# Two graph layers on one core: sums by a stationary identity instead of accumulated transposes

## The chip, the core and the metric

The kernel runs on one core of a Trainium2 chip. The metric is the device time in microseconds (us) of one launch. Every line number below is a line of the kernel before, as its profile gives it. The engines are called PE (TensorE's matmuls), PEld (TensorE's weight loads), DVE (VectorE), ACT (ScalarE), POOL (GpSimd) and SP (SyncE).

## The reference

The input x has 8 batches of 2048 nodes with 256 features; adj is a symmetric 2048 x 2048 matrix, nearly all zero, with ones on the diagonal. Two layers follow each other, each with a residual and a layer norm around it. Cut to what matters:

```python
# layer 0, four heads of 64, keys in chunks of 256
q, k, v = x @ Wq.T + bq, x @ Wk.T + bk, x @ Wv.T + bv
scores = clip(einsum(q, k) / sqrt(64), -10, 10)
scores = where(mask == 0, -10, scores)
attn = softmax(scores)                 # within each chunk of 256 keys
ctx = sum over chunks of attn @ v
out = layernorm(ctx @ Wo.T + bo + x) * gamma + beta
x = layernorm(x + out)
# layer 1, four heads of 64
Wh = x @ W
e = leaky_relu(s_src[i] + s_dst[j]);  alpha = softmax(where(adj, e, -inf))
x = layernorm(x + elu(alpha @ Wh))
```

## The kernel before

The kernel makes use of the few ones in adj. A first part builds, for each node, the list of its neighbours, sorts the nodes by the number of neighbours and cuts them into NT = 16 tiles of 128 nodes. Tile t is processed with CAPS[t] neighbour slots: 24, 14, 13, 12, 11, 11, 10, 10, 9, 9, 8, 8, 7, 7, 6, 5, in all 164. A slot is one neighbour of each of the 128 nodes; its rows are fetched by one indirect DMA (`gather`, line 489, issued by POOL). Two slots lie together in a unit, a buffer of a ring of 14; a tile with an odd number of slots has a last unit with one slot. The 16 tiles have 86 units.

Layer 0 works on G = 2 batches at a time, so there are four groups g, and 64 pairs of group and tile. For each pair:

- `scores0` multiplies the gathered keys with the node's own query row. For about a third of the units VectorE both multiplies and reduces (`reduced`, lines 554 and 556). For the others (62 of a group's 86 units, 248 in all) VectorE multiplies (line 547), with the product laid out as NJ = 8 pieces of 2 slots x 64 columns, and TensorE adds the eight pieces by eight accumulating transposes into the bank `pr` (line 566). ScalarE copies that to `prT` (lines 572 and 574) and a matmul with the 0/1 matrix `sel` (line 576) adds the remaining 8 values of each slot and head, back in the layout of nodes by slots, into a bank `tf`.
- `softmax0` clamps the scores (line 590 from `tf`, line 593 for those that VectorE made) and turns them to weights `al`.
- `context0` multiplies the gathered values by the weights, on VectorE (line 501) or for the last quarter of the units on ScalarE (line 507), and `summed` (line 514) adds all slots by accumulating transposes, four of 128 x 128 a slot, into a bank `acc`, which ScalarE copies to `cT` (line 626).
- `finish0` multiplies by Wo (line 635) and does the norms; `rows1` transposes the rows (line 307, bank `tf`, copied to `x1T` by line 658) and makes layer 1's table (line 663). `tables` makes the next group's tables of queries, keys and values (lines 336 to 391, banks `tk`).

Layer 1 works on pairs of groups, four batches at once, so there are 32 pairs of p and tile, and each slot is summed in two halves k of 512 columns. `softmax1` makes the weights, `context1` multiplies and sums as in `context0`, into two banks `acc`, and copies both to `hT` (line 722). `finish1` transposes `hT` back (line 734, bank `mf`), takes the exponential (line 737) and the rest of elu (lines 738 and 741), and does the norm. The result is scattered by POOL (lines 748 and 753) in the step after.

The order is written out in a list `seq`: layer 0 of groups 0 and 1, then groups 2 and 3 with one tile of layer 1's first pair after every second tile, then the second pair alone. The first pair's tiles come with 7, 6, 9, 10, 11, 24, 10, 8, 7, 5, 8, 9, 11, 14, 13 and 12 slots, the second pair's with 5, 7, 8, 9, 10, 11, 12, 14, 24, 13, 11, 10, 9, 8, 7 and 6. A step's functions are called in the order scores0 of this tile, then (where one is due) finish1 of the last and context1 of the next tile of layer 1, then rows1, finish0, tables, softmax0 and context0. A planner places each engine's instructions from there, so those of neighbouring functions lie between each other; where they share a buffer, the order of the calls holds.

PSUM has eight banks of 128 x 512 f32. Before, they go to `acc` 2, `tf` 2, `tk` 2, `pr` 1 and `mf` 1.

Of the kernel before, what the change touches and what calls it, by code (L numbers as in the profile page):

```python
# [45 lines left out]
def edge_lists(tc: tile.TileContext, pool, bank, adj, const, ident, rec_d, B, between):  # L46
# [24 lines left out]
    for it in range(NT):  # L71
# [8 lines left out]
        if it % 4 == 0:  # L80
            kp = bank("acc")
# [92 lines left out]
def sparse_path(ctx: ExitStack, tc: tile.TileContext, keep, x, adj, Wq, bq, Wk, bk, Wv, bv, Wo, bo, gamma, beta, W, a,  # L174
# [38 lines left out]
    def by_part(v):  # L213
        return v.rearrange("p (j h d) -> p h j d", h=H, d=DP)


    sel = const.tile([P, P // DP], F32, name="sel")
    nc.gpsimd.memset(sel, 1.0)
    nc.gpsimd.affine_select(out=sel, in_=sel, compare_op=ALU.is_ge, fill=0.0, base=0, pattern=[[-DP, P // DP]],
                            channel_multiplier=1)  # L220
    nc.gpsimd.affine_select(out=sel, in_=sel, compare_op=ALU.is_ge, fill=0.0, base=DP - 1, pattern=[[DP, P // DP]],
                            channel_multiplier=-1)
# [9 lines left out]
    def bank(tag, bufs=2):  # L232

        return ps.tile([P, 512], F32, tag=tag, name=tag, bufs=bufs)
# [296 lines left out]
    def scores0(g, t):  # L531
# [6 lines left out]
        ps_sc = bank("tf")[:, 0:GH * S].rearrange("p (s e) -> p s e", e=GH)  # L538
# [21 lines left out]
        for i in range(1, npe, 4):  # L560
            some = units[i:min(i + 4, npe)]
            pr = bank("pr", 1).rearrange("p (k r) -> p k r", r=P)
            for k, (u, s0, n) in enumerate(some):
                prod = product(i + k)
                for j in range(NJ):
                    nc.tensor.matmul(pr[0:n * W8, k, :], prod[:, j // (NJ // UNIT), j % (NJ // UNIT), :], ident, is_transpose=True,  # L566
                                     start=(j == 0), stop=(j == NJ - 1), skip_group_check=True)
            m = len(some)
            prT = work.tile([P, 4, P], F32, tag="prT", name="prT", bufs=1)
            full = m - 1 if some[-1][2] < UNIT else m  # L570
            if full:
                nc.scalar.copy(prT[:, 0:full, :], pr[:, 0:full, :])
            if full < m:
                nc.scalar.copy(prT[0:W8, full, :], pr[0:W8, full, :])
            for k, (u, s0, n) in enumerate(some):
                nc.tensor.matmul(ps_sc[:, s0:s0 + n, :], prT[0:n * W8, k, :], sel[0:n * W8, 0:n * GH],  # L576
                                 start=(s0 == UNIT), stop=(k == m - 1 and i + m == npe), skip_group_check=True)
        for unit in units[npe:]:
            reduced(*unit)
        st0[g, t] = ps_sc, sc, min(S, UNIT * npe)  # L580
# [5 lines left out]
    def softmax0(g, t):  # L586
        S = CAPS[t]
        n = GH * S
        ps_sc, sc, sp = st0.pop((g, t))
        nc.vector.tensor_scalar(sc[:, :, UNIT:sp], ps_sc[:, UNIT:sp, :].rearrange("p s e -> p e s"), -10.0, 10.0, op0=ALU.max,  # L590
                                op1=ALU.min)
        for some in [sc[:, :, 0:UNIT]] + ([sc[:, :, sp:]] if sp < S else []):
            nc.vector.tensor_scalar(some, some, -10.0, 10.0, op0=ALU.max, op1=ALU.min)
# [16 lines left out]
    def context0(g, t):  # L610
# [3 lines left out]
        acc = bank("acc").rearrange("p (c r) -> p c r", r=P)  # L614
# [38 lines left out]
    def rows1(g, t):  # L653

        o = st0.pop((g, t))
        pt = transposed(o.rearrange("p b f -> p (b f)"), "tf", 2)
# [13 lines left out]
    got1, st1 = {}, {}  # L670

# [31 lines left out]
    def context1(p, t):  # L703
# [3 lines left out]
        accs = [bank("acc").rearrange("p (c r) -> p c r", r=P) for _ in range(2)]  # L707
# [5 lines left out]
        for i, (u, s0, n) in enumerate(units):  # L713
            for k in range(2):
# [3 lines left out]
                summed(accs[k], part, s0 == 0, s0 + n == S)  # L718
        hTs = []
        for k in range(2):  # L720
            hT = work.tile([P, G * KC, P], F32, tag="hT", name="hT")
            nc.scalar.copy(hT, accs[k])
            hTs.append(hT)
        xr = work.tile([P, 2, GF], F32, tag="xr", name="xr")
        nc.sync.dma_start(xr, x1_d[p][t * P:(t + 1) * P])
        st1[p, t] = hTs, xr

    def finish1(p, t):
        hTs, xr = st1.pop((p, t))
        sums = small.tile([P, 2 * G], F32, tag="sums1", name="sums1")  # L730
        for k, hT in enumerate(hTs):
# [79 lines left out]
    for k, (layer, i) in enumerate(seq):  # L811
# [6 lines left out]
        if layer == 0:  # L818
# [15 lines left out]
            if tables_first:  # L834
                fetch(k + 1)
# [451 lines left out]
```

## Time and profile before

| | |
|---|---|
| runs shown | 2379.63, 2385.73, 2388.16 us; median 2385.73 us |
| profiled execution | 2397.55 us, its span 2395.8 us |
| mean granted TensorE clock | 0.885 |
| busy: PE, DVE, ACT, POOL | 1900.4, 1833.5, 1409.0, 1505.0 us |
| DMA | 669.10 MB, mean 279 GB/s |

The busy time of an engine is the time in which at least one of its instructions runs. TensorE's matmuls overlap each other, so the mean duration of one (some 290 ns for a transpose) is longer than the distance from one to the next. The granted clock is the share of TensorE's full clock that its throttle let through. The span falls into stages: preparation and the neighbour lists to about 210 us, the first steps of layer 0 to about 440, layer 0 of groups 0 and 1 to about 1090, group 2 with layer 1 and the last projections to about 1448, group 3 with layer 1 to about 1952, and layer 1 alone to the end.

### The profile page before, as it was taken

The numbers are of one execution on the slowest core, as the hardware profiler recorded it, in microseconds if no ns is written. First come the engines' busy times: TensorE is split into PE (matmuls) and PEld (weight loads), VectorE is DVE, ScalarE is ACT, GpSimd is POOL, SyncE is SP. The second block draws the span as 40 slices with busy tenths as digits, with TensorE's granted clock in tenths as the row PEclk, the third lists the DMA queues.
The fourth block names the chain that finished last, engine by engine and source line by source line (L and its number), as shares of the span: only waits on it lengthen the run. The fifth ranks groups of instructions, "written<-read, shape, count | busy, mean of one in ns | idle before, by whom it ended". The sixth has DMA issues, their size and how long they took to land. (4 is left out here: it accounts for less than half of the span.)

```text
span 2395.8 us, 38844 instructions
## 1 busy us (share of the span) xinstructions
PE 1900.4 (79%) x11946; PEld 1622.0 (68%) x11946; DVE 1833.5 (77%) x4099; ACT 1409.0 (59%) x5036; POOL 1505.0 (63%) x1230
## 2 busy tenths in 40 slices
PE   7686889889899898999988885888678786664764
PEld 5565677778778787777876774776566675554653
DVE  6864587877588988588988886887788887775775
ACT  4573455546566555655565665664356677665766
POOL 3125455672666676376668856774677685787883
PEclk9897899899999999999998997987878987877887
DMA  7737877795889798598879977896679896786884
GB/s 259 242 137 272 265 270 281 260 346 209 316 287 320 260 334 319 212 388 298 302 258 353 360 281 238 285 321 221 230 274 326 306 319 248 278 310 231 302 296 154
DMA packets 239982, 669.10 MB, mean 279 GB/s; under 512 B 43688, under 2 KB 70059, under 8 KB 237719
## 3 DMA queue, kind: packets, MB, share of 16 engines
q0 software_dynamic: 156800, 505.01, 60.1%
q1 hardware_dynamic: 79248, 151.55, 17.2%
q10 hardware_dynamic: 3718, 9.97, 1.3%
q8 instruction: 98, 1.61, 0.3%
q14 instruction: 118, 0.96, 0.1%
HBM read 612.79 MB, written 126.36 MB: 309 GB/s over the span
## 5 line engine op out<-in xcount | busy, mean ns | idle before, releaser
L489 POOL DMA_INDIRECT u<-kv_d,idx x656 | 810.2, 1235 | 436.4 <-PE acc L514 185.7
L514 PE MATMUL acc<-ident,u 128*128 128x128 f32 x5248 | 713.4, 291 | 157.0 <-DVE u L501 89.0
L514 PEld LDWEIGHTS acc<-ident,u 128*128 128x128 f32 x5248 | 637.5, 151 | 220.7 <-DVE u L501 133.2
L489 POOL DMA_INDIRECT u<-wh_d,idx x328 | 416.5, 1270 | 148.2 <-issue 76.4
L566 PE MATMUL pr<-ident,u 128*128 128x128 f32 (+1 forms) x1984 | 287.0, 295 | 78.7 <-DVE u L547 77.2
L501 DVE TENSOR_TENSOR u<-u,al 128x1024 f32<-128x1024 f32 x280 | 334.5, 1234 | 1.5
L566 PEld LDWEIGHTS pr<-ident,u 128*128 128x128 f32 (+1 forms) x1984 | 245.4, 151 | 110.8 <-DVE u L547 104.6
L547 DVE TENSOR_TENSOR u<-u,qx 128x1024 f32<-128x1024 f32 (+1 forms) x248 | 302.0, 1218 | 18.3 <-DMA u<-kv_d,idx 15.1
L501 DVE TENSOR_TENSOR u<-u,z 128x1024 f32<-128x1024 f32 x266 | 314.4, 1212 | 0.6
L507 ACT ACTIVATE u<-u,z 128x64 f32<-128x64 f32 x1008 | 262.0, 337 | 25.0 <-DVE z L700 17.1
L507 ACT ACTIVATE u<-u,al 128x64 f32<-128x64 f32 x800 | 209.1, 342 | 23.2 <-DVE al L607 22.3
L663 PE MATMUL mf<-wa,x1T 128*128 128x264 f32 x512 | 167.6, 455 | 23.1 <-ACT x1T L658 14.8
L351 POOL TENSOR_TENSOR xt<-xt,beta_r 128x1024 f32<-128x1024 f32 x32 | 77.1, 2410 | 143.1 <-PE tk L336 126.3
L385 PE MATMUL tk<-wq,xT 128*128 128x256 f32 x512 | 145.2, 397 | 24.4 <-ACT kvs L379 24.4
L451 ACT ACTIVATE nm<-sums 128x2 f32<-128x2 f32 (+1 forms) x160 | 32.4, 202 | 221.3 <-DVE sums L641 122.6
L372 PE MATMUL tk<-wkv,xT 128*128 128x256 f32 x512 | 151.7, 410 | 12.9 <-ACT xC L341 12.6
L635 PE MATMUL mf<-wo,cT 128*128 128x256 f32 x512 | 148.4, 415 | 6.3 <-ACT whs L666 5.3
L376 PE MATMUL tk<-wkv,xC 128*128 128x256 f32 x512 | 144.5, 399 | 0.0
L663 PEld LDWEIGHTS mf<-wa,x1T 128*128 128x128 f32 x512 | 101.7, 218 | 59.7 <-ACT x1T L658 23.6
L455 ACT ACTIVATE sq<-o,nm 128x256 bf16<-128x256 f32 x256 | 129.7, 507 | 5.3
L554 DVE TENSOR_TENSOR u<-u,qx 128x1024 f32<-128x1024 f32 (+1 forms) x96 | 116.0, 1214 | 16.6 <-DMA qx<-qx_d,node 7.1
L590 DVE TENSOR_SCALAR sc<-tf 128x64 f32<-128x64 f32 (+5 forms) x64 | 14.0, 218 | 138.2 <-PE tf L576 138.2
(168 smaller groups left out, 3254.0 us busy)
## 6 DMA issues: line engine op xcount, KB each, us to landing
kv_d<-kvs SPq DMA_DIRECT2D x48, 512.0 KB, 6.0
wh_d<-whs SPq DMA_DIRECT2D x64, 260.0 KB, 5.8
xt<-in_x_dram SPq DMA_DIRECT2D x64, 256.0 KB, 4.8
qx_d<-xt SPq DMA_DIRECT2D x32, 512.0 KB, 4.4
qx_d<-qs SPq DMA_DIRECT2D x64, 256.0 KB, 5.8
x_d<-o SPq DMA_DIRECT2D x64, 256.0 KB, 5.2
xr<-x_d SPq DMA_DIRECT2D x32, 512.0 KB, 4.9
u<-kv_d,idx POOLq DMA_INDIRECT x656, 6.5
```

Source lines behind the costliest of these rows:

```text
L372: nc.tensor.matmul(pm[:, 0:F], xT[:, b * KC + kc, rows], wkv[:, kc, 0:F], start=(kc == 0), stop=False, skip_group_check=True)
L376: nc.tensor.matmul(pm[:, F:], xC[:, b * KC + kc, rows], wkv[:, kc, F:], start=False, stop=(kc == KC - 1), skip_group_check=True)
L385: nc.tensor.matmul(qb, xT[:, b * KC + kc, rows], wq[:, kc, :], start=(b == 0 and kc == 0), stop=False, skip_group_check=True)
L455: nc.scalar.activation(sq, src[:, k, :], AF.Square, bias=nm[:, k:k + 1], accum_out=m2[:, k:k + 1])
L489: nc.gpsimd.indirect_dma_start(out=u[:, k, 0:width], out_offset=None, in_=table, in_offset=bass.IndirectOffsetOnAxis(ap=idx[:, t, s0 + k:s ...
L501: nc.vector.tensor_tensor(pv, pv, av, op=ALU.mult)
L507: nc.scalar.activation(pe, pe, AF.Copy, scale=al[:, e, s0 + k:s0 + k + 1])
L514: nc.tensor.matmul(acc[:, c, :], part[:, k, c * P:(c + 1) * P], ident, is_transpose=True, start=first and k == 0 and c == 0, stop=last and ...
L547: nc.vector.tensor_tensor(prod.rearrange("p k j (s w) -> p k j s w", w=W8), u[:, :, 0:GF].rearrange("p s (k j w) -> p k j s w", k=UNIT, w=W8),
L566: nc.tensor.matmul(pr[0:n * W8, k, :], prod[:, j // (NJ // UNIT), j % (NJ // UNIT), :], ident, is_transpose=True, start=(j == 0), stop=(j ...
L635: nc.tensor.matmul(po[:, b, :], cT[:, b * KC + kc, :], wo[:, kc, :], start=(b == 0 and kc == 0), stop=False, skip_group_check=True)
L663: nc.tensor.matmul(pw[:, 0:F + 2 * H], xT[:, b * KC + kc, :], wa[:, kc, :], start=(kc == 0), stop=(kc == KC - 1))
```

## The change

Both kinds of sums change from accumulated transposes (the data stationary, the identity moving) to plain matmuls with the identity stationary and the data moving, which leave the sum untransposed.

- Scores: the eight pieces of a unit are added by eight matmuls of 128 columns (64 for a unit with one slot) into the unit's own columns of a bank `pr`, up to four units side by side. The copies `prT`, the matrix `sel` and its matmul are gone. In `softmax0` VectorE adds the remaining 8 values straight from PSUM, one `tensor_reduce` for each bank, into `sc`; one clamp for the whole tile takes the place of two or three.
- Layer 1: a slot's half of 512 columns is added by one matmul. The banks are left as they are until `finish1`, which reads them where it read `mf`; the copies `hT` and the transposes of line 734 are gone, and the exponential has a buffer of its own.
- Layer 0's context sums (`summed` from `context0`) stay as they were.
- PSUM: `acc` has one bank, which `rows1` uses too; `tf` is gone; `pr` has two; `a1` is new with two, for layer 1's sums. While group 3 runs and after it, when `tables` no longer needs `tk`, layer 1's tiles use `a1` and `tk` in turn.

The diff, without the lines that only move a bank of the preparation and remove `sel`:

```diff
@@ -535,7 +529,7 @@
         sc = small.tile([P, GH, S], F32, tag="sc", name="sc")
 
         npe = 1 + len(units) - len(units) // 3
-        ps_sc = bank("tf")[:, 0:GH * S].rearrange("p (s e) -> p s e", e=GH)
+        sums = []
         W8 = GH * DP
         qv = q.rearrange("p (k j w) -> p k j w", k=UNIT, w=W8).unsqueeze(3)
 
@@ -559,25 +553,18 @@
         reduced(*units[0])
         for i in range(1, npe, 4):
             some = units[i:min(i + 4, npe)]
-            pr = bank("pr", 1).rearrange("p (k r) -> p k r", r=P)
+            ns = sum(n for _, _, n in some)
+            pr = bank("pr")
             for k, (u, s0, n) in enumerate(some):
                 prod = product(i + k)
+                part = pr[:, k * UNIT * W8:(k * UNIT + n) * W8]
                 for j in range(NJ):
-                    nc.tensor.matmul(pr[0:n * W8, k, :], prod[:, j // (NJ // UNIT), j % (NJ // UNIT), :], ident, is_transpose=True,
-                                     start=(j == 0), stop=(j == NJ - 1), skip_group_check=True)
-            m = len(some)
-            prT = work.tile([P, 4, P], F32, tag="prT", name="prT", bufs=1)
-            full = m - 1 if some[-1][2] < UNIT else m
-            if full:
-                nc.scalar.copy(prT[:, 0:full, :], pr[:, 0:full, :])
-            if full < m:
-                nc.scalar.copy(prT[0:W8, full, :], pr[0:W8, full, :])
-            for k, (u, s0, n) in enumerate(some):
-                nc.tensor.matmul(ps_sc[:, s0:s0 + n, :], prT[0:n * W8, k, :], sel[0:n * W8, 0:n * GH],
-                                 start=(s0 == UNIT), stop=(k == m - 1 and i + m == npe), skip_group_check=True)
+                    nc.tensor.matmul(part, ident, prod[:, j // (NJ // UNIT), j % (NJ // UNIT), :], start=(k == 0 and j == 0),
+                                     stop=(k == len(some) - 1 and j == NJ - 1), skip_group_check=True)
+            sums.append((some[0][1], ns, pr))
         for unit in units[npe:]:
             reduced(*unit)
-        st0[g, t] = ps_sc, sc, min(S, UNIT * npe)
+        st0[g, t] = sc, sums
 
 
     ebuf = const.tile([P, GH * TOP + 1], F32, name="ebuf")
@@ -586,11 +573,11 @@
     def softmax0(g, t):
         S = CAPS[t]
         n = GH * S
-        ps_sc, sc, sp = st0.pop((g, t))
-        nc.vector.tensor_scalar(sc[:, :, UNIT:sp], ps_sc[:, UNIT:sp, :].rearrange("p s e -> p e s"), -10.0, 10.0, op0=ALU.max,
-                                op1=ALU.min)
-        for some in [sc[:, :, 0:UNIT]] + ([sc[:, :, sp:]] if sp < S else []):
-            nc.vector.tensor_scalar(some, some, -10.0, 10.0, op0=ALU.max, op1=ALU.min)
+        sc, sums = st0.pop((g, t))
+        for s0, ns, pr in sums:
+            nc.vector.tensor_reduce(sc[:, :, s0:s0 + ns].rearrange("p e s -> p s e"),
+                                    pr[:, 0:ns * GH * DP].rearrange("p (s e d) -> p s e d", e=GH, d=DP), axis=AX.X, op=ALU.add)
+        nc.vector.tensor_scalar(sc, sc, -10.0, 10.0, op0=ALU.max, op1=ALU.min)
         e = ebuf[:, 0:n]
         ev = e.rearrange("p (e s) -> p e s", s=S)
         nc.scalar.activation(ev, sc, AF.Exp)
@@ -611,7 +598,7 @@
         S = CAPS[t]
         al = st0.pop((g, t))
         units = got0[g, t][1]
-        acc = bank("acc").rearrange("p (c r) -> p c r", r=P)
+        acc = bank("acc", 1).rearrange("p (c r) -> p c r", r=P)
 
         na = len(units) // 4
         if g == PG:
@@ -653,7 +640,7 @@
     def rows1(g, t):
 
         o = st0.pop((g, t))
-        pt = transposed(o.rearrange("p b f -> p (b f)"), "tf", 2)
+        pt = transposed(o.rearrange("p b f -> p (b f)"), "acc", 1)
         xT = work.tile([P, G * KC, P], F32, tag="x1T", name="x1T", bufs=1)
         nc.scalar.copy(xT, pt)
         wh = work.tile([P, WW], F32, tag="whs", name="whs")
@@ -668,6 +655,7 @@
 
 
     got1, st1 = {}, {}
+    turns, made = [0], [False]
 
     def fetch1(p, t):
         got1[p, t] = gather(2 * WW, wh_d[p], idx1, t)
@@ -704,7 +692,9 @@
         S = CAPS[t]
         e = st1.pop((p, t))
         units = got1.pop((p, t))
-        accs = [bank("acc").rearrange("p (c r) -> p c r", r=P) for _ in range(2)]
+
+        turns[0] += 1
+        accs = [bank("tk" if made[0] and turns[0] % 2 else "a1") for _ in range(2)]
         na = len(units) // 4, (len(units) + 2) // 4
         for i, (u, s0, n) in enumerate(units):
             for k in range(2):
@@ -715,25 +705,18 @@
                 part = u[:, :, k * WW:k * WW + GF]
                 if i < len(units) - na[k]:
                     weighted(part, e[:, k * GH:(k + 1) * GH], s0, n)
-                summed(accs[k], part, s0 == 0, s0 + n == S)
-        hTs = []
-        for k in range(2):
-            hT = work.tile([P, G * KC, P], F32, tag="hT", name="hT")
-            nc.scalar.copy(hT, accs[k])
-            hTs.append(hT)
+                for s in range(n):
+                    nc.tensor.matmul(accs[k], ident, part[:, s], start=s0 + s == 0, stop=s0 + s == S - 1)
         xr = work.tile([P, 2, GF], F32, tag="xr", name="xr")
         nc.sync.dma_start(xr, x1_d[p][t * P:(t + 1) * P])
-        st1[p, t] = hTs, xr
+        st1[p, t] = accs, xr
 
     def finish1(p, t):
-        hTs, xr = st1.pop((p, t))
+        accs, xr = st1.pop((p, t))
         sums = small.tile([P, 2 * G], F32, tag="sums1", name="sums1")
-        for k, hT in enumerate(hTs):
-            ph = bank("mf", 1)
-            for c in range(G * KC):
-                nc.tensor.transpose(ph[:, c * P:(c + 1) * P], hT[:, c, :], ident)
-
-            ex = hT.rearrange("p c r -> p (c r)")
+        for k, ph in enumerate(accs):
+
+            ex = work.tile([P, GF], F32, tag="ex", name="ex")
             nc.scalar.activation(ex, ph, AF.Exp)
             nc.vector.scalar_tensor_tensor(xr[:, k], ph, 0.0, xr[:, k], op0=ALU.max, op1=ALU.add)
             for b in range(G):
@@ -831,6 +814,7 @@
                 finish0(*at(i - 1))
             if g + 1 < NG:
                 tables(g + 1, i % NT)
+            made[0] = g + 1 == NG
             if tables_first:
                 fetch(k + 1)
             softmax0(g, t)
```

## Prediction

> **What bounds the kernel now.** I read the page's first section, then the windows view cut at the stages, then each engine's waits. The chain that ended last says nothing here, because it holds only the last store. The page's first line shows three engines near 80%, so no average settles it:
>
> ```profile
> PE 1900.4 (79%) x11946; PEld 1622.0 (68%) x11946; DVE 1833.5 (77%) x4099; ACT 1409.0 (59%) x5036; POOL 1505.0 (63%) x1230
> ```
>
> The windows view of the first layer-0 steps, of layer 0 with projections, of groups 2 and 3 with layer 1 between, and of layer 1 alone (columns: us, busy us and count of PE, PEld, DVE, ACT, POOL, then clock, DMA share, GB/s):
>
> ```profile
> 210.00:440.00 230.00, 192.22 (x1161) 163.36 (x1162) 168.26 (x305) 115.46 (x395) 128.91 (x109) 0.88 0.80 274
> 440.00:1090.00 650.00, 585.75 (x3742) 500.90 (x3742) 504.14 (x1013) 377.46 (x1458) 402.46 (x316) 0.95 0.83 297
> 1090.00:1448.00 358.00, 317.38 (x2136) 275.09 (x2135) 301.84 (x621) 217.26 (x802) 251.85 (x192) 0.95 0.87 311
> 1448.00:1952.00 504.00, 377.56 (x2380) 324.11 (x2380) 402.92 (x892) 285.63 (x1047) 350.51 (x278) 0.83 0.80 278
> 1952.00:2396.00 444.00, 272.56 (x1820) 234.41 (x1820) 313.39 (x759) 301.72 (x1073) 310.44 (x250) 0.79 0.73 263
> ```
>
> See PE at 90% and 89% from 440 to 1448 at clock 0.95: there TensorE sets the pace. It is at 75% from 1448 with DVE at 80%, and at 61% in the tail, where POOL is at 70% and issues one gather per 1.30 us, pauses included. Busy us times clock is TensorE's work at full speed: 169, 556, 302, 313 and 215 us, or 74, 86, 84, 62 and 48% of the windows. I take 86% as the most that this program gets out of TensorE.
>
> What a sum costs is in TensorE's timeline (start, us, line, count). A run of n lasts the spacing times n-1, plus one latency (0.27 us at 128 columns, 0.38 us at 256):
>
> ```profile
> 944.27 0.84 PE L576 MATMUL tf<-sel,prT 128*128 128x16 f32 x6
> ...
> 946.99 1.03 PE L376 MATMUL tk<-wkv,xC 128*128 128x256 f32 x4
> ...
> 960.88 3.00 PE L514 MATMUL acc<-ident,u 128*128 128x128 f32 x26
> 963.71 1.36 PE L566 MATMUL pr<-ident,u 128*128 128x128 f32 x11
> ```
>
> The transposing sums (L514, L566) follow each other every 0.109 us at 128 columns, the plain matmul L376 every 0.216 us at 256 columns, and L576, with 16 columns only, still every 0.11 us[...]. So a moving column costs about 0.84 ns in both kinds. The groups hold the decisive difference, the count:
>
> ```profile
> L376 PE MATMUL tk<-wkv,xC 128*128 128x256 f32 x512 | 144.5, 399 | 0.0
> L576 PE MATMUL tf<-sel,prT 128*128 128x16 f32 (+1 forms) x496 | 73.7, 271 | 32.5 <-ACT prT L572 31.4 <-ACT prT L574 0.3
> L336 PE MATMUL tk<-ident,xt 128*128 128x128 f32 x256 | 45.9, 306 | 21.2 <-DMA xt<-in_x_dram 9.4 <-ACT qs L389 5.9 <-ACT kvs L379 5.7
> ```
>
> Line 376 is called 64 x 2 x 2 = 256 times and is recorded 512 times; line 576 is called 248 times (once per unit) and recorded 496. The transposing line 336 is called 32 x 2 x 4 = 256 times and recorded 256. **A plain f32 matmul is two instructions, a transposing one is one.** The same holds of lines 372, 385, 635 and 663 against 307, 313, 514, 566 and 734.
>
> [...]
>
> **The change, part by part** (at full clock).
> (a) Layer 1's sums. Line 514 has 5248 transposes, half of them layer 1's: 2624 x 0.109 = 286 us go. In their place come 328 slots x 2 = 656 calls with 512 moving columns, no row of which exists here. By the two-instruction rule [...]563 us in all: **+277**. Bounds: 0.429 each if an identity were not doubled (-5 us)[...]. I take 0.858.
> (b) Scores. 1984 instructions become 3968 of 0.109 us: **+216**. The odd units' 64-column ones are taken at the same price[...]; half of that would save 17 us. Line 576 goes: -496 x 0.112 = **-56**.
> (c) Line 734's transposes go: -256 x 0.109 = **-28**. TensorE in all: **+409 us**.
> (d) ScalarE loses the copies prT (L572, L574: 41 us) and hT (35 us). It is at 59%; nothing is gained where TensorE leads.
> (e) VectorE gains 76 reductions from PSUM over 30464 elements. From line 556's slope, 1.035 ns an element and 0.15 us each: 43 us (41 to 86). The clamps L590 and L593 (14 + 16 us) give way to one per tile (14 us). Net +27 us, 0.4 us a step, under TensorE's cover to 1448. If that cover were gone, it would cost its 27 us.
> (f) Waits. In the tail TensorE's 45.6 us of waiting for line 738 to release the single bank mf, and the two copies in that chain, go; what is late next is POOL's gathers, which already fill it. The sums now hold their banks until finish1 of the next layer-1 tile has read them. With two banks a1 the next context1 waits for that Exp and two VectorE passes (0.6 + 2 x 0.68 us); behind it queue all later matmuls. From group 3 on, two more banks alternate. The context's bank acc is single now and shared with rows1, so its transposes queue behind the copy cT (0.58 us): 0 to 20 us in all, taken inside the shares below.
> (g) No DMA is added, moved or removed on SP or POOL. But POOL's line 489 waits for line 514 to free ring units (220 us in all), so slower sums delay gathers. The memset and selects of sel in the preparation are nothing.
>
> By window, from the counts of lines 566, 576 and 734 in it and layer 1's slots there (43, 82 and 203): scores add 25, 65, 32, 40 and 0 us; sums add 0, 0, 36, 69 and 171; line 734 takes 0, 0, 4, 7 and 17. TensorE's full-speed work becomes 194, 621, 366, 415 and 369 us. At 86% that needs 226, 722, 426, 483 and 429 us against windows of 230, 650, 358, 504 and 444.
>
> So 440 to 1090 is over by 72. Of this 20 are covered: TensorE waits there 22.3 us for products and 5.7 us for prT, because a unit's product takes 1.22 us and its eight sums 0.87, and they will take 1.74. **+52.** The next window is over by 68, less 10 for its waits (10.7 us for products): **+58.** The other three are just under the limit. Cover that thin leaks: I take half of the 25 in the first (**+12**), a quarter of the 102 in the fourth (**+25**) and a tenth of the 154 in the tail (**+15**), where POOL leads and hT's chain goes. Sum **+162 us**. The profiled execution took 2397.6 us (span 2395.8), 0.5% above the median of the three runs, 2385.7; on the median that gives **2548 us**.
>
> **Rivals.**
> *The sums become the tail of every step.* In context1 VectorE makes a two-slot part in 1.22 us and TensorE sums it in 0.87; it will need 1.72, so a tile of ten slots ends 17.2 us after its first product and not 11.9. If finish1 and the ring wait for that, the last two windows pay all of theirs, about 102 + 107 us (5.7 a tile over 19 tiles), and the others 60 + 50 + 25: +344, 2730 us. For it: DVE idles 64 us for gathers in the tail. Against: the next tile's first product comes later than that end.
> *Good cover.* Leaks are nothing, the two full windows pay 45 + 35, and the tail gains 15 from hT's chain: +65, 2451 us. For it: clocks of 0.83 and 0.79 in the last windows, which a busier TensorE would raise; that is already in my full-speed sums.
> *Not doubled.* If a matmul with the identity were one instruction, (a) is -5 and (b) -56: TensorE loses 89 us, of which perhaps 40 count, 2346 us, **faster**. It decides at the count: 656 and 1984 records, not 1312 and 3968. Against it stands every plain line of this trace; it is also the case in which the change does what a shorter instruction list suggests.
>
> **How the numbers follow.** Forecast 0.57 (2490 to 2620), tail of sums 0.20, good cover 0.17, not doubled 0.06. The range 2450 to 2660 leaves out the last and the upper part of the second. A measurement here tells about 0.5% from no change. Faster 0.06, same 0.02, slower 0.92.
>
> **What would show it.** The score line with 3968 records at 0.109 us, layer 1's with 1312 at 0.43 us; PE busy near 2200 us or more; PEclk up in the last two windows; layer 0 (440 to 1448 now) longer by about 110 us; no rows for sel, prT and hT; reductions of about 0.68 us at 512 elements. Single records, or a layer 0 of unchanged length, would make the prediction wrong.

## The result, and the profile after

The change makes the kernel slower. The median of its runs is 2522.04 us (2498.49 to 2531.26, four runs), that of the kernel before beside it 2382.68 us (2378.05 to 2388.16, four runs): a ratio of **1.0569, interval 1.0486 to 1.0651** (here and below the ratio is the one on record for all runs of a comparison, which differs by up to 0.3% from the quotient of the two medians). The profiled execution took 2529.34 us, its span 2527.5 us, at a mean granted clock of 0.94 (0.885 before). Lines that begin with L in this section are lines of the kernel after: 562 is the score sum (566 before), 709 layer 1's sum, 508 the context sum (514 before), 483 the gather (489 before).

The page of the kernel after, its first part and three rows of its groups (line, engine, operation, output and input, count | busy us, mean ns of one | idle us before them):

```profile
PE 2188.6 (87%) x11866; PEld 1663.4 (66%) x11866; DVE 1876.7 (74%) x4087; ACT 1346.3 (53%) x4876; POOL 1484.0 (59%) x1227
...
L562 PE MATMUL pr<-u,ident 128*128 128x128 f32 (+1 forms) x3968 | 497.2, 284 | 61.7 <-DVE u L541 61.5
...
L709 PE MATMUL a<-u,ident 128*128 128x512 f32 x772 | 353.7, 611 | 22.0 <-DVE u L495 15.7
...
L709 PE MATMUL tk<-u,ident 128*128 128x512 f32 x540 | 247.8, 614 | 25.9 <-DVE u L495 24.0
```

The counts carry the most. 1984 calls of line 562 are 3968 records, and 656 calls of line 709 are 772 + 540 = 1312. Since a slot's half is now one call and not four, TensorE has 80 records fewer than before, and is busy 288 us longer.

The windows view of the kernel after, cut where the same tiles end their context sums as at 460, 1087, 1448 and 1952 us before (columns: us, busy us and count of PE, PEld, DVE, ACT, POOL, then clock, DMA share, GB/s):

```profile
210.00:462.00 252.00, 217.11 (x1461) 192.63 (x1462) 191.41 (x327) 120.79 (x433) 145.84 (x118) 0.93 0.78 263
462.00:1149.00 687.00, 624.82 (x4242) 555.93 (x4240) 494.88 (x984) 345.80 (x1353) 371.48 (x303) 0.97 0.76 274
1149.00:1562.00 413.00, 378.54 (x2250) 302.92 (x2248) 318.40 (x642) 212.81 (x800) 249.97 (x196) 0.97 0.79 276
1562.00:2080.00 518.00, 441.34 (x2363) 326.41 (x2364) 415.80 (x885) 271.94 (x1007) 349.77 (x278) 0.92 0.78 270
2080.00:2527.50 447.50, 375.66 (x846) 164.02 (x844) 311.84 (x739) 283.38 (x1023) 305.67 (x248) 0.92 0.73 258
```

For the kernel before, the last two rows of the windows in the prediction stand; its first three at these cuts are:

```profile
210.00:460.00 250.00, 209.20 (x1270) 177.97 (x1271) 185.47 (x330) 130.78 (x458) 143.76 (x118) 0.87 0.80 272
460.00:1087.00 627.00, 567.40 (x3624) 485.15 (x3623) 483.94 (x987) 360.55 (x1391) 384.77 (x307) 0.96 0.83 299
1087.00:1448.00 361.00, 318.75 (x2148) 276.22 (x2145) 304.84 (x622) 218.84 (x807) 254.69 (x193) 0.95 0.87 311
```

Read the length of each row, after its window, against before's 250, 627, 361, 504 and 444: by the copies cT of the 9th, 36th, 48th and 64th pair the five stretches grew by 2, 60, 52, 14 and 4 us. The two in which TensorE was already at 90% pay nearly all. (The second ends four tiles into group 2, whose first is the 33rd pair.) In the last two TensorE does 93 and 131 us more work at full speed, the clock rises from 0.83 and 0.79 to 0.92, and the time hardly moves. Busy time by clock is now 202, 606, 367, 406 and 346 us, or 80, 88, 89, 78 and 77% of the stretches. Summed, and set against the same cut of before (1558 us), TensorE does 369 us more.

TensorE's timeline of the kernel after (start, us, line, count):

```profile
1019.10 3.18 PE L562 MATMUL pr<-u,ident 128*128 128x128 f32 x27
...
2299.75 13.90 PE L709 MATMUL a<-u,ident 128*128 128x512 f32 x32
```

With one latency at the end (the median record of line 562 lasts 0.275 us, that of line 709 0.592 us), 27 records of 128 columns in 3.18 us are 0.11 us apart; 32 of 512 columns in 13.90 us are 0.43 us apart, so a call of line 709, two records, costs 0.86 us.

VectorE's groups of the kernel after, one of the seven shapes of the new reduction; all seven together are 76 instructions and 43.5 us:

```profile
L578 DVE TENSOR_REDUCE sc<-pr 128x64 f32<-128x512 f32 x36 | 24.7, 686 | 24.6 <-PE pr L562 24.6
```

The waits of POOL in the kernel after (us in total, times, longest):

```profile
POOL u L483 <- PE acc L508: 310.9, 91, 18.4
```

It is the wait for the context sums to free units of the ring; before it was 220.3 us. VectorE's wait for gathered rows of layer 1's tables, which later gathers would lengthen, was 80.5 us before and is now:

```profile
DVE z L668 <- DMA u<-wh_d,idx: 123.0, 52, 9.5
```

No row is left for sel, prT and hT. VectorE's wait for the score sums, on the way to the softmax, has become shorter. First before, then after:

```profile
DVE sc L590 <- PE tf L576: 138.2, 54, 11.2
```

```profile
DVE sc L578 <- PE pr L562: 83.0, 39, 10.0
```

### The profile page after: what moved, and what is told of

The parts are those of the page before. It is cut to its first block, busy times and chain, and to the rows that moved or that the text cites. A ratio compares the mean times of both kernels' runs of the same rounds, so it can differ in the third digit from the quotient of the medians.

```text
span 2527.5 us, 38414 instructions
## 1 busy us (share of the span) xinstructions
PE 2188.6 (87%) x11866; PEld 1663.4 (66%) x11866; DVE 1876.7 (74%) x4087; ACT 1346.3 (53%) x4876; POOL 1484.0 (59%) x1227
## 5 line engine op out<-in xcount | busy, mean ns | idle before, releaser
L483 POOL DMA_INDIRECT u<-kv_d,idx x656 | 798.8, 1218 | 521.1 <-PE acc L508 247.5
L562 PE MATMUL pr<-u,ident 128*128 128x128 f32 (+1 forms) x3968 | 497.2, 284 | 61.7 <-DVE u L541 61.5
L562 PEld LDWEIGHTS pr<-u,ident 128*128 128x128 f32 x3968 | 482.9, 200 | 84.0 <-DVE u L541 76.5
L508 PE MATMUL acc<-ident,u 128*128 128x128 f32 x2624 | 336.0, 280 | 61.2 <-DVE u L495 56.4
L709 PE MATMUL a<-u,ident 128*128 128x512 f32 x772 | 353.7, 611 | 22.0 <-DVE u L495 15.7
L508 PEld LDWEIGHTS acc<-ident,u 128*128 128x128 f32 x2624 | 297.4, 144 | 94.4 <-DVE u L495 81.8
L541 DVE TENSOR_TENSOR u<-u,qx 128x1024 f32<-128x1024 f32 (+1 forms) x248 | 294.5, 1187 | 69.2 <-DMA u<-kv_d,idx 61.2
L501 ACT ACTIVATE u<-u,z 128x64 f32<-128x64 f32 x1008 | 257.6, 337 | 38.8 <-DVE z L688 38.7
L709 PEld LDWEIGHTS a<-u,ident 128*128 128x128 f32 x772 | 147.9, 196 | 194.3 <-issue 155.3
L709 PE MATMUL tk<-u,ident 128*128 128x512 f32 x540 | 247.8, 614 | 25.9 <-DVE u L495 24.0
L709 PEld LDWEIGHTS tk<-u,ident 128*128 128x128 f32 x540 | 104.2, 197 | 154.2 <-issue 113.0
```

What stands on the lines that cost most here:

```text
L483: nc.gpsimd.indirect_dma_start(out=u[:, k, 0:width], out_offset=None, in_=table, in_offset=bass.IndirectOffsetOnAxis(ap=idx[:, t, s0 + k:s ...
L501: nc.scalar.activation(pe, pe, AF.Copy, scale=al[:, e, s0 + k:s0 + k + 1])
L508: nc.tensor.matmul(acc[:, c, :], part[:, k, c * P:(c + 1) * P], ident, is_transpose=True, start=first and k == 0 and c == 0, stop=last and ...
L541: nc.vector.tensor_tensor(prod.rearrange("p k j (s w) -> p k j s w", w=W8), u[:, :, 0:GF].rearrange("p s (k j w) -> p k j s w", k=UNIT, w=W8),
L562: nc.tensor.matmul(part, ident, prod[:, j // (NJ // UNIT), j % (NJ // UNIT), :], start=(k == 0 and j == 0), stop=(k == len(some) - 1 and j ...
L709: nc.tensor.matmul(accs[k], ident, part[:, s], start=s0 + s == 0, stop=s0 + s == S - 1)
```

## The experiments

The theory on trial was that of the prediction: a plain f32 matmul costs two instructions, and in the two stretches that TensorE paces this extra work is the loss. Its first rivals put the loss on the banks, or on VectorE's new reductions; the order of the instructions came up on the way. Ratios are to the kernel before in the same comparison, with 95% intervals. Where the time went is told by the five stretches: what each grew over the kernel before, in us, from the same copies cT in one profiled execution each.

| kernel | ratio | start to 9th | to 36th | to 48th | to 64th | to the end |
|---|---|---|---|---|---|---|
| after | 1.057 | +2 | +60 | +52 | +14 | +4 |
| scores_only | 1.035 | -4 | +58 | +15 | +4 | +6 |
| sums_only | 1.027 | +1 | +4 | +17 | +29 | +11 |
| before_plain | 1.114 | +5 | +88 | +70 | +50 | +65 |
| f32r | 1.030 | +6 | +69 | +7 | +11 | -15 |
| plain_old_order | 1.108 | +17 | +36 | +66 | +68 | +64 |
| old_plain_order | 1.106 | -1 | +84 | +72 | +41 | +48 |
| f32r_order | 1.048 | +17 | +79 | +16 | +6 | -8 |
| one_pass | 1.022 | -5 | +59 | +0 | -6 | -9 |
| before_banks | 1.006 | +5 | +5 | +9 | -1 | -5 |
| before_tl | 1.119 | +5 | +148 | +62 | +19 | +48 |
| after_tl | 1.195 | +1 | +234 | +61 | +109 | +57 |
| f32r_tl | 1.162 | +4 | +221 | +32 | +86 | +30 |

**One half of the change at a time.** First the scores alone, layer 1 as before:

```diff
-nc.tensor.matmul(pr[0:n * W8, k, :], prod[...], ident, is_transpose=True, ...)
+nc.tensor.matmul(part, ident, prod[...], ...)
...
+nc.vector.tensor_reduce(sc[...], pr[...], axis=AX.X, op=ALU.add)
```

> The scores' part alone: the kernel before with the new scores (eight plain matmuls by a stationary identity a unit, VectorE's reduction from PSUM, two banks pr, no prT and no sel) and layer 1's sums as they were, with two banks acc as before and one bank tf for rows1. Passes theory (the loss is TensorE's extra passes, paid where TensorE is full): the two windows before layer 1 pay as in the whole change, about 62 us, the third pays half of its 52, the fourth some 6, the tail nothing: +93 us, ratio 1.039 (1.025 to 1.050); PE busy up by some 200 us, record count of the score line 3968. Banks theory (the loss is the single acc and banks held until finish1): within 1% of before, as both stay away here. VectorE theory (the loss is its new reductions on the way to the softmax): all of the loss, 1.05 to 1.06.

Measured: 2473.14 us, 1.0351 (1.0329 to 1.0374). The number is that of the theory, and the loss lies where the scores are. Then layer 1's sums alone:

```diff
-summed(accs[k], part, s0 == 0, s0 + n == S)
+for s in range(n):
+    nc.tensor.matmul(accs[k], ident, part[:, s], start=s0 + s == 0, stop=s0 + s == S - 1)
```

> Layer 1's part alone: the changed kernel with the scores of before (transposes, prT, sel; one bank pr, one bank tf), so acc is single and shared with rows1, and layer 1's sums are plain matmuls of 512 columns that keep their banks until finish1. Passes theory: nothing before layer 1 starts, half of the third window's 52 us, some 8 in the fourth, 4 in the tail: +39 us, ratio 1.016 (1.005 to 1.030); 1312 records of the sum line at 0.43 us. Banks theory: nearly all of the loss, 1.04 to 1.06, and part of it before layer 1 starts. VectorE theory: within 0.5% of before.

Measured: 2456.32 us, 1.0274 (1.0246 to 1.0301): within what was expected, above its centre. By stretch it is less good: 17, 29 and 11 us in the last three, where 26, 8 and 4 were expected, so most of this loss lies where TensorE had room. The halves add up to 6.2%, the whole is 5.7%.

**Passes without anything else of the change.** In the kernel before, the word is_transpose is dropped from the score sums and from layer 1's sums. The data stays stationary and the identity moves, so the result, banks, copies and gathers are the same, and only the number of passes doubles; 1984 x 0.109 + 2624 x 0.109 = 502 us of TensorE are added.

```diff
-matmul(pr[0:n * W8, k, :], prod[...], ident, is_transpose=True, ...)
+matmul(pr[0:n * W8, k, :], prod[...], ident, ...)
```

> The kernel before with one thing altered: the transposes of the scores and of layer 1's sums are issued as plain f32 matmuls (transpose mode off), the data still stationary. The results, banks, copies and VectorE's work are those of before. Passes theory: 1984 + 2624 calls become two instructions each, +216 + 286 = +502 us of TensorE's time at 0.109 us, none of it given back by removed work, so it is slower than the change: 80 + 66 us in the windows where TensorE is full, some 25 + 20 in the last two: +190, ratio 1.08 (1.06 to 1.11). Banks and VectorE theories: within 0.5% of before.

Measured: 2660.7 us, 1.1135 (1.1112 to 1.1158), a little above the range expected. The two full stretches lost 88 and 70 us where 80 and 66 were expected, the last two 50 and 65 where some 25 and 20 were. The groups of this kernel show the rule with the operands in their old places (5248 + 2624 = 7872):

```profile
L514 PE MATMUL acc<-ident,u 128*128 128x128 f32 x7872 | 951.7, 280 | 28.2 <-DVE u L501 26.7
...
L566 PE MATMUL pr<-ident,u 128*128 128x128 f32 (+1 forms) x3968 | 495.1, 284 | 52.7 <-DVE u L547 52.7
```

**The change without the second pass.** Both new sums of the kernel after read their operands as float32r, a type of the same size, in which the products and gathered rows are now written: the page has `u<-u,qx 128x1024 fp32r<-128x1024 f32` for line 544 (those lines of the edit are left out here):

```diff
-nc.tensor.matmul(accs[k], ident, part[:, s], ...)
+nc.tensor.matmul(accs[k], identr, part[:, s].bitcast(F32R), ...)
```

> The whole change with the operands of the two new sums typed float32r, the products and gathered rows rounded to that format by whatever writes them; everything else as in the change. This leaves out the low part of the products in the two sums. Passes theory: one instruction a call, 1984 and 656 records instead of 3968 and 1312. If such a pass takes 0.43 us for 512 columns, TensorE has 89 us less work than before and the time is 0.985 of before (0.965 to 0.995), the case of the prediction that ended faster; if it takes 0.22, some 0.96. Banks theory: still 1.04 or more. VectorE theory: still 1.02 to 1.06, as the reductions stay.

Measured: 2465.4 us, 1.0304 (1.0273 to 1.0335). **This is a miss** for the theory of passes, and where the theory of VectorE's reductions (1.02 to 1.06) put it. TensorE got what the edit promised, as the groups of this kernel show, one record a call:

```profile
L565 PE MATMUL pr<-u,identr 128*128 128x128 f32 (+1 forms) x1984 | 334.9, 327 | 105.2 <-DVE u L544 100.8
...
L712 PE MATMUL a<-u,identr 128*128 128x512 f32 x386 | 173.2, 575 | 100.5 <-DVE u L498 95.6
```

In this kernel TensorE is busy 1821.7 us at clock 0.803, against 1900.4 us at 0.885 before: at full speed some 220 us less, as 1900.4 x 0.885 and 1821.7 x 0.803 are 1682 and 1463. Yet the kernel is 3% slower than before. The second stretch still loses 69 us, now with TensorE waiting for products (105 us of idle time ahead of L565). So something besides second passes came with the change. The kernel leaves the placing of instructions in each engine's queue to a planner, and the order changed in parts that were never edited too: POOL issues the same 1144 indirect DMAs in the kernel before and in the kernel after, none of them edited, and at 113 of the 1144 places, from the 79th on, one of another tile stands. The next four runs put the order on trial.

**The order held, the passes changed, and the reverse.** Each engine's order is fixed by a chain of dependencies in the program, which adds no instruction to TensorE (x11946 in the first page below, as in the kernel before). First the kernel before with the order that was planned for before_plain:

```diff
+    for a, b in zip(names, names[1:]):
+        tc.add_manual_dep(traced[b], a, info, reason="order")
```

> The kernel before, every instruction as it was, but each engine issues in the order that the planner made for before_plain, the kernel with the same sums as plain matmuls (a chain of issue-order edges imposes it). Order theory (a plan made for dear matmuls is itself a bad one, and float32r inherited it): the losses that after, before_plain and float32r share at the same tiles of groups 0 and 1 come back here with cheap transposes, 60 to 90 us, ratio 1.025 to 1.04. Passes theory: within 1% of before. Banks and VectorE theory: within 1% of before.

Measured: 2644.03 us, 1.1059 (1.0996 to 1.1123), far above both expectations. Its page and POOL's waits:

```profile
PE 1938.2 (73%) x11946; PEld 1688.0 (64%) x11946; DVE 1851.9 (70%) x4099; ACT 1416.5 (54%) x5036; POOL 1456.4 (55%) x1230
```

```profile
POOL u L489 <- PE acc L514: 475.9, 117, 22.6
```

TensorE's and VectorE's counts, and those of ScalarE and POOL, are those of the kernel before; no engine is busy above 73%. In the traces VectorE, ScalarE and POOL go through the same sequence of operations as in before_plain. The wait for ring units has more than doubled from 220.3 us. **The order alone is worth 10% here**, with what the chain itself costs inside it (see below). Then before_plain with the order of the kernel before (the diff of before_plain and the chain):

> before_plain (the sums of the scores and of layer 1 as plain f32 matmuls, everything else as before), but each engine issues in the order of the kernel before. It carries the 502 us of passes and no new order. Passes theory: as before_plain, 1.10 to 1.125. Order theory: the part that the order cost is gone, 1.06 to 1.09.

Measured: 2648.96 us, 1.1077 (1.1015 to 1.1139), in total as the theory of passes said. Its page and POOL's waits:

```profile
PE 2316.8 (88%) x16554; PEld 2109.3 (80%) x16554; DVE 1830.4 (69%) x4099; ACT 1414.2 (53%) x5036; POOL 1476.0 (56%) x1230
```

```profile
POOL u L489 <- PE acc L514: 444.2, 130, 17.5
```

**The passes alone, in the old order, are worth 10% as well.** But they don't lie where the theory has them: of the 251 us of the table only 102 are in the second and third stretch, 132 in the last two, and in the second TensorE does 629 us of full-speed work in 664 us (busy 635.5 us at clock 0.99), a share of 95%. Each cause is enough by itself, and they don't add: with both (before_plain) it is 11.4%. Both show the same wait of POOL. The two kernels differ in TensorE (73% busy against 88%), so this wait is a symptom that they share and doesn't tell which of the two is at work. No kernel was run with its own order imposed, so what the chain costs is not measured. It can hardly be the 10%: f32r_order, below, has the chain and is at 1.048, and before_tl has another order without any chain and is at 1.119.

**Is the 3% of f32r its order?** First f32r under an order that was planned for bf16 sums:

```diff
+    fixed_order(tc)
```

> The float32r kernel (the change with one cheap instruction a call), but each engine issues in the order that the planner makes when the same calls are bf16 matmuls[...]. The products and gathered rows are rounded to float32r in the two sums. Order theory: the 78 us by which float32r was slower than before go and the 220 us less of TensorE's work show where it was full, ratio 0.95 to 0.98. Banks or VectorE theory: it stays at 1.02 to 1.04, since the banks, the reductions and the removed copies are the same.

Measured: 2507.69 us, 1.0482 (1.0421 to 1.0544), above what either theory said. Then the kernel after with sums that read the high half of each value as bf16 (a 16-bit type), in the order that the planner makes for it:

```diff
-nc.tensor.matmul(accs[k], ident, part[:, s], ...)
+nc.tensor.matmul(accs[k], identb, high(part[:, s]), ...)
```

> The change with the operands of the two new sums read as bf16 (the high half of each f32 word, every second bf16 element), so each call is one pass; banks, reductions and everything else as in the change. This leaves out the low half of the products in the sums. Order theory and passes theory: 0.95 to 0.98 of before, about as f32r_order. Banks or VectorE theory: 1.02 to 1.04.

Measured: 2440.58 us, 1.0219 (1.0159 to 1.0278), a miss for order and passes, and within what banks or reductions would give. Its page:

```profile
PE 1623.1 (67%) x9226; PEld 1209.5 (50%) x9226; DVE 1869.6 (77%) x4088; ACT 1336.9 (55%) x4876; POOL 1481.2 (61%) x1227
```

TensorE is at 67% and all engines have room, but the second stretch is 59 us longer than before. The sequence of operations on VectorE, ScalarE and POOL is that of f32r_order, so these two, 67 us apart, differ in the type of the sums and in the chain, not in the order. Score sums no longer than those of the kernel before don't win this stretch back, in any of these three kernels.

**The banks alone.** The kernel before with the change's PSUM: acc single and shared with rows1, a1 with two banks for layer 1's sums, tf single.

```diff
-acc = bank("acc").rearrange("p (c r) -> p c r", r=P)
+acc = bank("acc", 1).rearrange("p (c r) -> p c r", r=P)
...
-pt = transposed(o.rearrange("p b f -> p (b f)"), "tf", 2)
+pt = transposed(o.rearrange("p b f -> p (b f)"), "acc", 1)
...
-accs = [bank("acc").rearrange("p (c r) -> p c r", r=P) for _ in range(2)]
+accs = [bank("a1").rearrange("p (c r) -> p c r", r=P) for _ in range(2)]
```

> The kernel before with the change's bank layout alone: acc has one bank, shared with rows1's transposes; layer 1's sums get two banks a1 of their own (still transposed, copied to hT and transposed back); tf has one bank for the scores. The planner orders it anew. Banks theory: most of what float32r still lost, ratio 1.02 to 1.04. Passes theory: within 1% of before. Order theory (any new plan of this program is worse than that of before, whatever is changed): 1.01 to 1.04, with the loss in layer 0's tiles 8 to 12, 16 to 20 and 24 to 28.

Measured: 2398.04 us, 1.0059 (1.0034 to 1.0083), 13 us. The layout of the banks is a small part of the loss. The copies hT stay in this kernel, so it doesn't hold layer 1's banks until `finish1`; f32r and one_pass do, and their last stretch is 15 and 9 us shorter than before.

**Another planner's model throughout.** If the order matters so much, does the change lose only by the luck of its order? The planner is given a different model of the machine, in the kernel before, in the kernel after and in f32r:

```diff
-with _tile.TileContext(nc) as tc:
+with _tile.TileContext(nc, schedule_with_timeline_sim=True) as tc:
```

> The kernel before, nothing altered but the machine model by which the planner orders the instructions, so that all engines issue in another order. Order theory: another plan of the very same instructions costs a few per cent, 1.02 to 1.08. Passes and banks theories: within 1% of before.

> The changed kernel under that other machine model of the planner. Passes theory: slower than before_tl by some 5%, as with the usual plan, and never below before. Order theory: the difference between before_tl and after_tl is small, within 2%, as the plan and not the passes decides.

> The float32r kernel (one cheap instruction a call, operands rounded to that format) under the other machine model of the planner. If float32r lost to its plan alone, a plan made otherwise may let the 220 us less of TensorE's work show: 0.97 to 1.00 of before, and 5% or more below after_tl. If banks or VectorE's reductions were what it lost to, 1.02 or more again.

Measured: before_tl 2676.52 us, 1.1194 (1.1149 to 1.1239); after_tl 2856.81 us, 1.1954 (1.1905 to 1.2003); f32r_tl 2769.39 us, 1.1615 (1.1573 to 1.1657). The page of before_tl and its POOL waits:

```profile
PE 1940.3 (72%) x11946; PEld 1686.2 (63%) x11946; DVE 1866.4 (70%) x4099; ACT 1429.3 (53%) x5036; POOL 1501.3 (56%) x1230
```

```profile
POOL u L489 <- PE acc L514: 513.9, 94, 27.3
```

All three are worse than under the first model. before_tl lies beyond what even the order theory allowed; after_tl is slower than before_tl, as the theory of passes said; f32r_tl, above 1.02, is again where banks or reductions would put it. The comparison within the model is what counts: 1.1954 / 1.1194 = 1.068 for the change, 1.1615 / 1.1194 = 1.038 for the change without second passes, and so about 3% for the passes. Under the first model it was 1.057, 1.030 and 2.6%. For the whole span both the sign and the split repeat. By stretch they repeat in the second, where f32r_tl loses 73 us more than before_tl and f32r 69, and not in the fourth (67 against 11).

**Order or reductions, read from the traces.** No run left only the reductions out, but the traces tell how long their path is. VectorE's wait for the score sums in the second stretch (10th to 32nd pair), first in the kernel before, then in f32r:

```profile
DVE sc L590 <- PE tf L576: 40.1, 21, 5.6
```

```profile
DVE sc L581 <- PE pr L565: 10.4, 11, 2.7
```

From a tile's last score sum to its exponential, in the mean of the 10th to 36th pair, it is 3.0 us in the kernel before, 3.0 in scores_only, 3.6 in after, 2.3 in f32r_order and 2.7 in one_pass; only in f32r is it longer, 5.4. So the path through the reductions is about as short as that through prT, sel and the clamp was. VectorE's busy time in the second stretch grows by 9 to 29 us in these five, which are 58 to 79 us longer there. What has grown is the time for which a tile is in work, from its first product for TensorE (line 547) to the copy cT of its context, here beside what the second stretch lost (mean of the same pairs, us):

| kernel | first product to cT | stretch |
|---|---|---|
| before | 29.4 | |
| sums_only | 29.6 | +4 |
| before_banks | 29.7 | +5 |
| plain_old_order | 30.9 | +36 |
| scores_only | 38.5 | +58 |
| after | 38.7 | +60 |
| f32r | 39.2 | +69 |
| before_plain | 42.7 | +88 |
| old_plain_order | 43.0 | +84 |
| one_pass | 43.8 | +59 |
| f32r_order | 45.0 | +79 |

A tile holds its units of the ring until its context is summed. In the second stretch POOL waited 60 us for that in the kernel before, and 116 to 140 us in each of the last seven. This speaks for the order, in which the planner spreads a tile's work among that of its neighbours, and against the reductions as a delay of their own. It is two things seen together and not an experiment, and it doesn't say whether it is luck: sums_only and before_banks were planned anew too and lost only 4 and 5 us, while the kernels with the new scores lost 58 to 79 us in each of four plans by the first model, and 86 (after_tl) and 73 us (f32r_tl) against before_tl by the second.

## Why the prediction was right, and where its steps were not

The forecast was 2548 us (2450 to 2660) and slower; 2522 us came, 26 us below it. Point by point:

**The two-instruction rule** held: 3968 and 1312 records, at 0.11 and 0.43 us. The rival *not doubled* is out. Its number would not have come either: it gave 2346 us, faster, for single instructions. With single instructions the kernel took 2465 (f32r) and 2441 us (one_pass). The step that failed there is "TensorE loses 89 us, of which perhaps 40 count": the rest of the change cost more than the saved work brought, with TensorE at 74 and 67%.

**(a) to (c), the work of TensorE**: predicted +409 us at full speed, read from busy time and clock +369 us. The latter is good to some 20 us, as the clock is given to two places. By stretch it was +20, +61, +64, +93 and +131, predicted +25, +65, +64, +102 and +154 (the prediction cut the first two stretches at 440 and 1090 and not at 460 and 1087). As the counts and the spacings came as predicted, a part of the difference may lie in this way of reading. For the price of layer 1's call the rows of before are enough: two records of 512 columns at 0.84 ns a column, the spacing of lines 376 and 514, are an estimate of 0.86 us, and 0.86 came. The odd units' records of 64 columns, taken at the price of 128, came at that price too: line 562 has 0.112 us between two of either kind (median of the starts in the trace).

**The share of 86%** was low: the two full stretches run at 88 and 89%, and the second at 95% in plain_old_order. So it is not the most that TensorE can do there, but what it did in one order. At 95% the 606 us of the second stretch would need 638 and not 687.

**(d)** ScalarE lost 63 of 76 us and stands at 53%; no run tells whether anything was gained by that. **(e)** The reductions take 43.5 us (predicted 43), 0.686 us at 512 elements, where line 556 of before, from which they were estimated, took 0.682 (1.212 at 1024); the clamps went from 31 us to 16. Added up, VectorE's instructions take 27.6 us longer, predicted 27; its busy time, in which instructions that overlap count once, is 43 us longer. That this was covered in the two full stretches was argued, and no run removed the reductions alone.

**(f)** Banks, "0 to 20 us in all": 13 us in before_banks, which keeps the copies hT. One reading of the tail was too quick: 1.30 us a gather is POOL's pace in its quickest runs, and in the whole tail line 489 takes 224 us for 181 gathers, 1.24 us each without the pauses.

**(g)** POOL's wait for the sums grew from 220 to 311 us, and VectorE's wait for gathered rows from 80 to 123, the knock-on effect of which the step named the first half.

**By stretch**, predicted +12, +52, +58, +25 and +15, measured +2, +60, +52, +14 and +4. The two full ones are within 8 us. The other three were mis-sized, 52 us for what was 20: less leaked than the half, the quarter and the tenth that I let leak. So the rival *good cover* (2451) was near in these three and wrong in the two full ones; *sums become the tail* (2730, +102 and +107 at the end) is out, with 14 and 4 us there.

The number being right doesn't make every reason right. **What the runs show:** passes alone, in an order held fixed, are enough for a loss of this size (plain_old_order); taking the second pass out of the kernel after gives back 2.6% (1.0569 / 1.0304, f32r) to 3.4% (1.0569 / 1.0219, one_pass) of the 5.7; in the third stretch it gives back 36 to 52 of 52 us (f32r_order, f32r, one_pass), and there the reason given is supported, though another order without extra passes lost 72 us there too. **What they contradict:** in the second stretch the prediction put all of +52 on passes, and the kernel lost 60. f32r and one_pass lose 69 and 59 us there without extra passes, and the kernel before under another order 84 us with no edit at all. With the old order, doubled passes cost 36 us in this stretch. The right size there was the right number for a reason that these runs don't confirm, and so in part luck. What is missing in the prediction is a term for the new order that an edit brings, which can be as large as the whole effect (and as small as the 4 and 5 us of sums_only and before_banks), and of which a window of before shows nothing.

**What stays open:** the roughly 3% (2.2% in one_pass) that the change costs without its second passes. The layout of the banks is 0.6% of it. The rest is either the order or the new scores themselves, above all the path through the reductions (softmax0 can start a tile's clamp only when all reductions are done), and no experiment separates the two. By what was expected of them, f32r, one_pass and f32r_tl came out on the side of the banks or the reductions, and the banks alone are out. The traces speak for the order: the path is about as short as the old one in four of the five kernels looked at, and VectorE waits 83 us for the score sums where it waited 138. Whether another order of the same change would be quick is not known. The 2.6 to 3.4% given to the passes are not free of the order either, as each of these kernels was planned for itself. The kernel after in the order of the kernel before was not tried, as their instructions differ, nor was the change with its reductions left out. No version that was run beats the kernel before.

## What to carry to other kernels

Before replacing accumulated transposes by matmuls with a stationary identity, count records against calls: in this kernel a plain f32 matmul is two where a transpose is one (1984 calls were 1984 records in line 566 and are 3968 in line 562), and that is read in any row that already exists. Add the new work by stretch, and let only the stretches pay in which the engine is already near its ceiling; here the other three took in 244 us of work (20 + 93 + 131) for 20 us of time. That is no law: in plain_old_order the same three took in 325 us (34 + 123 + 168, busy time by clock again) and paid 149. Why they pay there and not here was not tried; in the change the copies hT and the transposes back are gone. Where a planner orders the queues, a time is that of the work and of a new order, so change one with the other held, or compare both kernels under a second plan, before a difference of some per cent is given a cause.

## What the runs showed of the hardware that I had not expected

A float32r matmul is one record (656 calls of line 712 are 386 + 270), and at 512 columns the records are about a quarter of a microsecond apart. TensorE's timeline of f32r in the tail (start, us, line, count, idle before):

```profile
2303.03 0.74 PE L712 MATMUL tk<-u,identr 128*128 128x512 f32 x2 [0.43 <-DVE u L498]
...
2314.57 3.74 PE L712 MATMUL tk<-u,identr 128*128 128x512 f32 x15 [0.41 <-DVE u L498]
2319.60 0.49 PE L712 MATMUL tk<-u,identr 128*128 128x512 f32 x1 [1.29 <-ACT u L504]
```

With the 0.49 us of a single one as latency, the fifteen in a row are 0.23 us apart and the two of a pair 0.25, against 0.43 us for one record and 0.86 us for the call of the same shape in f32. The idle 0.4 us ahead of each pair is TensorE waiting for VectorE's product: a call shorter by a factor of three and a half was worth little here, because TensorE then waited.

At 128 columns float32r brought nothing over the transposes. Eight score sums of f32r in a row take 1.11 us, eight transposes of line 566 took 1.05 us, and all 1984 keep TensorE busy for 334.9 us, against 287.0 us in the kernel before:

```profile
930.95 1.11 PE L565 MATMUL pr<-u,identr 128*128 128x128 f32 x8 [0.72 <-DVE u L544]
```

```profile
941.24 1.05 PE L566 MATMUL pr<-ident,u 128*128 128x128 f32 x8
```

With bf16 operands, in one_pass, the 1984 score sums are busy for 173.0 us:

```profile
L567 PE MATMUL pr<-u,identb 128*128 128x128 bf16 (+1 forms) x1984 | 173.0, 241 | 144.0 <-DVE u L546 134.6 <-DMA u<-kv_d,idx 7.7
```

What sets the distance at 128 columns was not shown.

And the granted clock moved with the load between the kernel before and the kernel after, as the prediction's signs had it: in the last stretch it rose from 0.79 to 0.92 as TensorE's busy time rose from 273 to 376 us, and over the whole span from 0.885 to 0.94 as its share rose from 79 to 87%. In f32r, with 74%, it was 0.803; but one_pass, with 67%, has 0.813, so the share alone doesn't give it. In the last stretch, then, a part of the added work was paid by the clock and not by time: 131 us more work at full speed, for 4 us of time.
